# A twelve-layer decoder on one core: masks on diagonal blocks in one attention, squares halved on GpSimd, context keys begun sooner, and two side streams that both move at each place

## The chip, the cores and the metric

The kernel runs on one core of one Trainium2 chip. The metric is device microseconds of one execution; lower is better. Engines are named as in the profile: PE (TensorE matmul), PEld (its weight loads), DVE (VectorE), ACT (ScalarE), POOL (GpSimd), SP (SyncE, which issues most DMAs).

## The reference

The input x is 8 batches of 256 rows of 256 numbers; a context of 8 x 77 rows goes with it. Four layers follow, each of an attention, a cross-attention over the context and a feed-forward part, and each part ends in `x = layernorm(x + part(x))`. Only these parts matter here:

```
L1 attention: 16 heads of 16, causal; softmax(mask(q k^T / 4)) v, then a projection
L2 ffn:       a shared expert and routed experts
L3 attention: a state-space block: rmsnorm, in-projection, a causal convolution of 4 taps,
              chunks with decay exp(cumsum), then
              y = rmsnorm(y * silu(z)) ; out = y @ Wo + residual
L3 cross:     q = softmax over each head's 16 numbers; k likewise over the context's keys;
              out = q + (q @ k^T v) / (q . sum k), then a projection
L3 ffn:       up (256 to 1024), gelu, down (1024 to 256); the butterflies are folded into up and down
```

## The kernel before

A builder class writes one straight program; a scheduler underneath then orders the instructions of each engine nearly as they were written, moving one ahead only where its model finds the engine free. Every engine then works through its queue in order. All big matmuls are `mm` (line 169 in the profile), whatever layer they belong to. `ps()` hands out one of 8 PSUM banks of 512 f32 columns.

**Pieces.** Work that is to lie beside other work is written as Python generators: each `yield` ends a piece. `later` queues a generator on `todo`, and `tick` takes its next piece. `side` takes pieces from two more queues, `sides[0]` and `sides[1]`; it is called at places that are written into the main thread by hand. Before, one call took one piece, from the two queues in turn, or from the one that had work.

**L1's attention** (`l1_attn`). For a batch, `shift` computes scores by queries to get each row's maximum: for query half t (0: 128 keys, 1: 256 keys) and groups g of heads, four banks `ps[j]` hold the scores of head rows j. `weights` computes them again by keys (key half c) for the exponents, `weigh` applies them to v. The causal mask is added by a matmul of constants in bf16. Before, it came first and covered all columns of the bank: `later` is 128 columns of zeros followed by the causal matrix, `unit` is an identity followed by zeros, both 256 wide. `mats(gs, n)` is four banks. At t = 1 and at c = 0 there are two groups a batch with two heads of 256 columns, at t = 0 and c = 1 one group with four heads of 128. L0's attention in the same kernel (`by_queries`, `by_keys`, lines 636 and 662) writes the mask last and on the diagonal block alone.

**The end of L2 and L3's keys** (`rest` in `l3_attn`). L2's shared expert for blocks 2 and 3 is 34 pieces. Between them come L3's context keys, one generator `l3_keys` a batch (a matmul, a softmax that goes over DVE, ACT, DVE and POOL, then two small matmuls a half and their masking). `key` begins batch b and ends batch b - 1. `need` at given pieces asks for the routed experts' results (gathers on POOL's DMA queue). `fill(n)` takes n pieces of `rest` between the first steps of L3's attention; `for _ in more` drains what is left after `inputs(0, ...)`.

**L3's loop** goes over the 8 batches b. A turn is `tick`, `weights(b)` (decay matrices: `sel` matmuls on line 2193, relu, G, exp, the transposes of line 2226 for xd), `inputs(b + 1)` (Wx matmuls, convolution on DVE, Wz matmuls, silu), then `outputs(b)` goes on `todo`. There are 14 places for `side` in a turn. `outputs` gates y by z, squares it on ACT (line 2261), sums the 512 squares of each row by matmuls with a column of ones (`onec`), takes the rsqrt, projects and norms; its last piece writes XT and queues `cross(b)` on `sides[0]`. `cross` is q and its softmax (`head_softmax`, lines 2438 to 2444), the transposes of q (2306), the product with the keys, a transpose back (2329), the projection with `renorm`, and the transposes of the new x (2349); its end queues `dense(b)` on `sides[1]`: four up pieces with gelu, two down pieces, and the last norm and the store. The text calls these c.q, c.qT, c.kv, c.oT, c.wp, c.xT and d.up0 to d.up3, d.down0 and d.down1, with the batch's number. After the loop, `while self.todo or ...` takes a `tick` and side pieces until nothing is left.

Of the kernel before, what the change touches and what calls it, by code (L numbers as in the profile page):

```python
# [20 lines left out]
P = 128  # L21
# [40 lines left out]
class Build:  # L62
    def __init__(self, tc, a, ctx):
        self.tc, self.nc, self.a = tc, tc.nc, a
        self.n = 0
        self.flip = 0
        pool = lambda name, bufs=1, **kw: ctx.enter_context(tc.tile_pool(name=name, bufs=bufs, **kw))
        self.const = pool("const")
        self.xp = pool("xp", 2)
        self.wp = pool("wp", 5)  # L70
        self.sm = pool("sm", 4)
        self.tmp = pool("tmp", 3)
        self.psp = pool("ps", 8, space=PSUM)
        self.dr = pool("dr", 1, space=DRAM)
        self.keep_stack = ctx.enter_context(ExitStack())
        self.open_keep = lambda: self.keep_stack.enter_context(tc.tile_pool(name="keep", bufs=1))
        self.keep = None
        self.X = [None] * NT
        self.XT = [None] * NBLK
        self.late = lambda: pool("late", side="right")  # L80
        self.l3w = None
        self.n_slot_sets = 0
        self.todo = []
        self.sides = [[], []]
        self.turn = 0
        self.l1kT = None
        self.results = None
        self.routed = None
        self.slots = {}
        self.ms = {}  # L90
# [12 lines left out]

    def side(self, n=1):

        for _ in range(n):
            live = [q for q in (self.sides[self.turn], self.sides[1 - self.turn]) if q]
            if not live:
                return
            self.turn ^= 1  # L110
            if next(live[0][0], self) is self:
                live[0].pop(0)

    def wave(self):

# [1147 lines left out]
    def l1_constants(self):  # L1263
        nc, pool = self.nc, self.l1s_pool

        mxps, vps = [self.t(pool, [P, 4, 4, 32], f"mxp{t}") for t in range(2)], []
        for m in mxps:
            nc.gpsimd.memset(m, 0.0)
        for n in range(2):
            v = self.t(pool, [P, 2, H, 32], f"vp{n}")  # L1270
            nc.gpsimd.memset(v, 0.0)
            nc.gpsimd.memset(v[:, :, :, 16:17], 1.0)
            vps.append(v)
        later = self.t(pool, [P, 2 * P], "later", BF)
        nc.vector.memset(later[:, :P], 0.0)
        nc.vector.tensor_copy(later[:, P:], self.causb)
        unit = self.t(pool, [P, 2 * P], "unit", BF)
        nc.vector.tensor_copy(unit[:, :P], self.identb)
        nc.vector.memset(unit[:, P:], 0.0)
        self.l1c = mxps, vps, later, unit  # L1280

    def l1_attn(self):
        nc, a = self.nc, self.a
        with ExitStack() as ctx:
# [4 lines left out]
            Wp = self.load_w(a["L1_attn_Wp"], 2, 256)  # L1289
            self.slot_rows(2)  # L1290
            bk, bq = self.fm("l1_bk"), self.fm("l1_bq")
            mxps, vps, later, unit = self.l1c
            rows = [slice(32 * j, 32 * j + 32) for j in range(4)]
            many = lambda m, n: m.unsqueeze(1).to_broadcast([P, n, m.shape[1]])
            mats = lambda gs, n: [self.ps()[:, : len(gs) * n].rearrange("p (g s) -> p g s", s=n) for j in range(4)]
# [30 lines left out]
            def shift(b, q, k):  # L1326

                q2 = self.t(w2, [P, 4, S], "q2", bufs=1)
                for t in range(2):
                    n = P * (t + 1)  # L1330
                    mxp = mxps[t]
                    for gs in ((0, 1, 2, 3),) if t == 0 else ((0, 1), (2, 3)):
                        ps = mats(gs, n)
                        for j in range(4):
                            nc.tensor.matmul(ps[j], self.identb, many(later[:, 2 * P - n :], len(gs)), start=True, stop=False)
                        for i, g in enumerate(gs):
                            for j, r in enumerate(rows):
                                nc.tensor.matmul(
                                    ps[j][:, i, :], q[r, g, t * P : (t + 1) * P], k[r, g, :n], start=False, stop=(g == gs[-1])
                                )  # L1340
                        for j in range(4):
                            self.mark = nc.vector.tensor_reduce(
                                mxp[:, gs[0] : gs[-1] + 1, j, 16], ps[j], AX.X, ALU.max, negate=True
                            )
                        self.tick()
                for t in range(2):
                    pt = self.ps().rearrange("p (g s) -> p g s", g=4)
                    for g in range(4):
                        nc.tensor.transpose(pt[:, g, :], mxps[t][:, g].rearrange("p j d -> p (j d)"), self.ident)
                    c = slice(t * P, (t + 1) * P)  # L1350
                    nc.vector.tensor_tensor(q2[:, :, c], pt, q[:, :, c], ALU.add)
                return q2

            def weights(q2, k):

                e = {}
                for c, gs in ((0, (0, 1)), (0, (2, 3)), (1, (0, 1, 2, 3))):
                    n = S - c * P
                    ps = mats(gs, n)
                    for j in range(4):  # L1360
                        nc.tensor.matmul(ps[j], self.causb, many(unit[:, :n], len(gs)), start=True, stop=False)
                    for i, g in enumerate(gs):
                        for j, r in enumerate(rows):
                            nc.tensor.matmul(
                                ps[j][:, i, :], k[r, g, c * P : (c + 1) * P], q2[r, g, c * P :], start=False, stop=(g == gs[-1])
                            )
                    o = self.t(w2, [P, 4, len(gs), n], "e", bufs=3)
                    for j in range(4):
                        nc.scalar.activation(o[:, j], ps[j], AF.Exp, scale=0.25)
                    for i, g in enumerate(gs):  # L1370
                        e[c, g] = o[:, :, i, :]
                    self.tick()
                return e
# [618 lines left out]
    def l3_attn(self):  # L1992
        nc, a = self.nc, self.a
        with ExitStack() as ctx:
# [6 lines left out]
            def rest():  # L2001

                keys, n, b = {}, 0, 0

                def key():
                    nonlocal b
                    if b < NB:
                        keys[b] = self.l3_keys(w4, b, Wkv, bkv, mask)
                        next(keys[b])
                        yield  # L2010
                    if b:
                        for _ in keys.pop(b - 1):
                            pass
                        yield
                    b += 1


                due = {(2, 8): 0, (2, 12): 1, (2, 16): 2, (3, 4): 3, (3, 8): 4, (3, 14): 5, (3, 16): 6}
                for blk in (2, 3):
                    for k, _ in enumerate(self.l2_shared(w4, blk, self.l2r)):  # L2020
                        if (blk, k) in due:
                            self.gates.append(self.mark)
                            self.need(due[blk, k])
                        yield
                        n += 1
                        if n >= 13 and n % 4 == 1:
                            yield from key()
                while b <= NB:
                    yield from key()
# [210 lines left out]
            def outputs(b, cv, zs, E, xd):  # L2240
# [18 lines left out]
                sq = zs  # L2259
                for h in (slice(0, 2), slice(2, 4)):  # L2260
                    nc.scalar.activation(sq[:, h, :], y[:, h, :], AF.Square)
                yield
                p2 = self.ps()
                for t in range(2):
                    self.mm(p2[:, t : t + 1], [(sq[:, c, t * P : (t + 1) * P], onec) for c in range(4)])
                r2 = self.t(self.sm, [P, 2], "r2")
                nc.vector.tensor_copy(r2, p2[:, :2])
                self.rsqrt(r2, r2, 1.0 / 512, 1e-5)
# [19 lines left out]
            def cross(b):  # L2288
# [9 lines left out]
                for t in two:  # L2298
                    x = self.X[2 * b + t]
                    nc.gpsimd.tensor_tensor(x, x, bp, ALU.add)  # L2300
                yield
                yield
                ps = self.ps()
                for t in two:
                    for k in range(2):
# [2 lines left out]
                        )  # L2308
                qT = self.t(w5, [P, 4, P], "qT", bufs=1)
                nc.scalar.copy(qT, ps.rearrange("p (k n) -> p k n", k=4))  # L2310
                yield
                for t in two:
                    ps = self.ps()[:, : 2 * 136].rearrange("p (g n) -> p g n", g=2)
                    for g in range(2):
# [3 lines left out]
                    for g in range(2):  # L2318
# [3 lines left out]
                            z[:, g, :].unsqueeze(2).to_broadcast([P, 8, 16]),  # L2322
                            ALU.mult,
                        )
                yield
                ps = self.ps()
                for t in two:
                    for k in range(2):
# [1 line left out]
                            ps[:, (2 * t + k) * P : (2 * t + k + 1) * P], q[:, t, k * P : (k + 1) * P], self.ident  # L2330
                        )
                nc.vector.tensor_tensor(qT, ps.rearrange("p (k n) -> p k n", k=4), qT, ALU.add)
                yield
                ps = self.ps()
                for t in two:
                    self.mm(ps[:, t * D : (t + 1) * D], [(qT[:, 2 * t + k, :], Wqp[:, k, 256:]) for k in range(2)])
                for t in two:
                    x = self.X[2 * b + t]
                    nc.vector.tensor_tensor(x, ps[:, t * D : (t + 1) * D], x, ALU.add)
                    renorm(2 * b + t)  # L2340
                yield
                yield
                if b % 2 == 0:
                    xts[b // 2] = self.t(self.xp, [P, 2, 512], "xt", bufs=5)
                at = xts[b // 2][:, :, (b % 2) * S : (b % 2 + 1) * S]
# [8 lines left out]

            def dense(b, xT):
                up, bu, wd = self.l3w
                for t in range(2):
                    x = self.X[2 * b + t]
                    nc.gpsimd.tensor_tensor(x, x, bc, ALU.add)
# [66 lines left out]
                self.side()  # L2426
            while self.todo or self.sides[0] or self.sides[1]:
                self.tick()
                self.side(2)


    def head_softmax(self, q, n):
# [590 lines left out]
```

## Time and profile before

| what | us |
|---|---|
| median of 3 executions | 3451.7 (3451.05 to 3453.99) |
| the profiled execution's own time | 3455.78 |
| its span, first to last instruction | 3454.1 |
| PE busy in the span | 3062.8 (89%) |
| POOL busy in the span | 918.5 (27%) |

Times in the profile count from the span's start. L1's attention lies from about 1079 to 1320 us, the shared expert's last pieces and the context keys from about 2905 to 3022, L3's loop from 3022.7; its turns begin at 3022.7, 3047.0, 3079.2, 3133.5, 3183.9, 3238.3, 3286.9 and 3327.8 (the `sel` matmuls of line 2193), and the tail after the last turn runs from about 3347 to the end. An instruction's line can be that of a helper; then the operands tell which step it is (`ps<-onec,zs` is the sum of squares). A granted clock of 1.00 is PE at full rate.

### The profile page before, as it was taken

The numbers are of one execution on the slowest core, as the hardware profiler recorded it, in microseconds if no ns is written. First come the engines' busy times: TensorE is split into PE (matmuls) and PEld (weight loads), VectorE is DVE, ScalarE is ACT, GpSimd is POOL, SyncE is SP. The second block draws the span as 40 slices with busy tenths as digits, with TensorE's granted clock in tenths as the row PEclk, the third lists the DMA queues.
The fourth block names the chain that finished last, engine by engine and source line by source line (L and its number), as shares of the span: only waits on it lengthen the run. The fifth ranks groups of instructions, "written<-read, shape, count | busy, mean of one in ns | idle before, by whom it ended". The sixth has DMA issues, their size and how long they took to land. (4 is left out here: it accounts for less than half of the span.)

```text
span 3454.1 us, 49695 instructions
## 1 busy us (share of the span) xinstructions
PE 3062.8 (89%) x19263; PEld 2187.0 (63%) x19274; DVE 1825.2 (53%) x4839; ACT 1084.6 (31%) x2426; POOL 918.5 (27%) x1371
## 2 busy tenths in 40 slices
PE   4777679989998998998999999998787999889887
PEld 2444357768886666675555777565555786567776
DVE  7887556641105656785111221576675443676663
ACT  4666422222222233332111111344222112235342
POOL 2222323343313211232000000331343453423232
PEclk6777779989999999998999999999787999879999
DMA  9900110025532000001010333100001562000000
GB/s 334 336 1 2 37 43 14 18 85 193 183 135 89 13 31 15 14 20 59 14 37 0 129 129 118 46 21 8 6 21 68 177 221 98 27 7 4 4 7 13
DMA packets 132657, 239.96 MB, mean 69 GB/s; under 512 B 14584, under 2 KB 104448, under 8 KB 124736
## 3 DMA queue, kind: packets, MB, share of 16 engines
q1 hardware_dynamic: 108160, 136.71, 11.9%
q0 software_dynamic: 23104, 98.95, 8.4%
q8 instruction: 156, 2.56, 0.3%
q10 hardware_dynamic: 1152, 1.05, 0.1%
q14 instruction: 85, 0.70, 0.1%
HBM read 156.98 MB, written 79.69 MB: 69 GB/s over the span
## 5 line engine op out<-in xcount | busy, mean ns | idle before, releaser
L169 PE MATMUL ps<-xt,w 128*128 128x256 f32 (+1 forms) x1408 | 444.4, 465 | 8.4 <-issue 8.4
L169 PE MATMUL ps<-w,hT 128*128 128x256 f32 (+1 forms) x1792 | 397.4, 379 | 0.0
L169 PEld LDWEIGHTS ps<-w,hT 128*128 128x128 f32 (+1 forms) x1792 | 329.9, 186 | 56.5 <-issue 6.0
L169 PE MATMUL ps<-gT,w 128*128 128x256 f32 (+1 forms) x1472 | 357.1, 401 | 5.7 <-ACT gT L157 3.0
L169 PEld LDWEIGHTS ps<-xt,w 128*128 128x128 f32 x1408 | 263.2, 194 | 150.3 <-issue 129.5
L169 PEld LDWEIGHTS ps<-gT,w 128*128 128x128 f32 x1472 | 276.3, 191 | 76.7 <-ACT gT L157 3.9
L169 PE MATMUL ps<-w,oT 128*128 128x256 f32 x704 | 165.8, 391 | 1.1 <-ACT oT L157 0.2
L169 PEld LDWEIGHTS ps<-w,oT 128*128 128x128 f32 x704 | 135.1, 195 | 34.0 <-issue 11.1
L1160 ACT ACTIVATE hT<-ps,more 128x256 f32<-128x256 f32 x152 | 72.1, 474 | 199.2 <-PE ps L169 199.2
L1171 DVE COPY y<-ps 128x512 f32<-128x512 f32 x41 | 28.3, 690 | 174.6 <-PE ps L169 174.6
L1237 DVE TENSOR_TENSOR hT<-hT,ps 128x512 f32<-128x512 f32 x56 | 38.6, 689 | 149.8 <-PE ps L169 149.4
L699 ACT ACTIVATE e<-ps,nm 128x128 bf16<-128x128 f32 (+1 forms) x256 | 104.0, 462 | 39.6 <-DVE nm L694 23.9
L289 POOL TENSOR_TENSOR xb<-x,rows 128x256 f32<-128x256 f32 x80 | 61.4, 774 | 190.7 <-DVE res L294 187.8
L277 DVE TENSOR_SCALAR x<-res,mv,rs 128x256 f32<-128x256 f32 x112 | 53.2, 475 | 109.9 <-POOL rs L197 109.9
L1233 ACT ACTIVATE hT<-ps 128x512 f32<-128x512 f32 x56 | 33.4, 597 | 237.7 <-PE ps L169 237.7
L249 PE MATMUL ps<-ident,x 128*128 128x128 f32 x288 | 56.4, 308 | 58.1 <-DVE x L277 43.2
L1730 POOL TENSOR_TENSOR kpad<-kpad,rows 128x256 f32<-128x256 f32 (+1 forms) x10 | 7.3, 730 | 363.5 <-DVE hu L1679 276.2
L983 PE MATMUL ps<-PT,V 77*64 77x256 f32 x512 | 93.8, 425 | 6.9 <-ACT PT L157 4.4
L916 POOL TENSOR_TENSOR P<-P,z 128x1232 f32<-128x1232 f32 (+1 forms) x32 | 55.2, 1736 | 167.6 <-DVE z L915 167.6
L1594 ACT ACTIVATE f<-ps,neg 128x512 f32<-128x512 f32 x128 | 77.4, 689 | 57.2 <-PE ps L1591 57.2
L1595 DVE SCALAR_TENSOR_TENSOR f<-ps,f 128x512 f32<-128x512 f32 x128 | 79.1, 680 | 25.7 <-ACT f L1594 25.7
L968 PEld LDWEIGHTS ps<-ident,P 128*77 128x77 f32 x512 | 59.4, 153 | 50.8 <-issue 23.8
(674 smaller groups left out, 6435.1 us busy)
## 6 DMA issues: line engine op xcount, KB each, us to landing
l2x<-zero SPq DMA_DIRECT2D x28, 1024.0 KB, 11.3
l0x<-zero SPq DMA_DIRECT2D x16, 1024.0 KB, 11.4
w<-in_L_ffn_rg SPq DMA_DIRECT2D x8, 1024.0 KB, 7.0
w<-in_L_ffn_ru SPq DMA_DIRECT2D x8, 1024.0 KB, 5.1
w<-in_L_ffn_rd SPq DMA_DIRECT2D x8, 1024.0 KB, 5.6
l2e<-y SPq DMA_DIRECT2D x22, 256.0 KB, 2.3
l0e<-y SPq DMA_DIRECT2D x19, 256.0 KB, 2.9
w<-in_L_xattn_Wk SPq DMA_DIRECT2D x4, 1024.0 KB, 4.9
```

Of the source, the lines that this page charges most:

```text
L169: self.nc.tensor.matmul(out, lhsT, rhs, start=(i == 0), stop=(i == last))
L249: self.nc.tensor.transpose(ps[:, k * P : (k + 1) * P], x[:, k * P : (k + 1) * P], self.ident)
L277: nc.vector.tensor_scalar(t, r, mv[:, 0:1], rs, ALU.subtract, ALU.mult)
L289: self.nc.gpsimd.tensor_tensor(t, self.X[i], row, ALU.add)
L699: nc.scalar.activation(e[:, : (t + 1) * P], ps[j][:, i, :], AF.Exp, bias=nm[:, t, h : h + 1], accum_out=z[:, t, h : h + 1],)
L916: eng.tensor_tensor(pr, pr, z.unsqueeze(2).to_broadcast([P, n, SC]), ALU.mult)
L968: nc.tensor.transpose(psv[:, m, t * P : (t + 1) * P], Pt[t][:, 2 * n + m, :], self.ident)
L983: nc.tensor.matmul(po[64 * m : 64 * m + 64, :S], V[:, h * 64 : (h + 1) * 64], ahead[n % 2][:, m, :], start=True, stop=True,)
L1160: nc.scalar.activation(hT[:, f + m, :], ps[:, m * 256 : (m + 1) * 256], func, bias=more[:, f + m : f + m + 1])
L1237: nc.vector.tensor_tensor(hT[:, f, :], hT[:, f, :], ps, ALU.mult)
L1594: nc.scalar.activation(f[:, j], ps[j], AF.Exp, bias=neg1)
L1595: self.mark = nc.vector.scalar_tensor_tensor(f[:, j], ps[j], 1.0, f[:, j], ALU.max, ALU.min)
```

## The change

Four edits that do not touch one another:

- `side` advances both queues by one piece at each place, and is called once in the final loop instead of taking two pieces. `cross` gets more empty pieces between its steps (14 pieces in all, where there were 8), `dense` one at its start (9 where there were 8).
- In `outputs`, GpSimd adds the second half of the squares to the first, and the matmuls with `onec` take two blocks of 128 where they took four.
- In `rest`, a key step follows every third piece of the shared expert from the 13th on, where it followed every fourth.
- In L1's attention the mask matmul comes last and covers only the block on the diagonal; `later` and `unit` go.

```diff
     def side(self, n=1):
-        for _ in range(n):
-            live = [q for q in (self.sides[self.turn], self.sides[1 - self.turn]) if q]
-            if not live:
-                return
-            self.turn ^= 1
-            if next(live[0][0], self) is self:
-                live[0].pop(0)
+        for q in self.sides * n:
+            if q and next(q[0], self) is self:
+                q.pop(0)
...
         # l1_attn, shift
-                        for j in range(4):
-                            nc.tensor.matmul(ps[j], self.identb, many(later[:, 2 * P - n :], len(gs)), start=True, stop=False)
                         for i, g in enumerate(gs):
                             for j, r in enumerate(rows):
                                 nc.tensor.matmul(
-                                    ps[j][:, i, :], q[r, g, t * P : (t + 1) * P], k[r, g, :n], start=False, stop=(g == gs[-1])
+                                    ps[j][:, i, :], q[r, g, t * P : (t + 1) * P], k[r, g, :n], start=(i == 0), stop=False
                                 )
+                        for j in range(4):
+                            nc.tensor.matmul(
+                                ps[j][:, :, t * P : n], self.identb, many(self.causb, len(gs)), start=False, stop=True
+                            )
...
         # l1_attn, weights
-                    for j in range(4):
-                        nc.tensor.matmul(ps[j], self.causb, many(unit[:, :n], len(gs)), start=True, stop=False)
...
+                    for j in range(4):
+                        nc.tensor.matmul(
+                            ps[j][:, :, :P], self.causb, many(self.identb, len(gs)), start=False, stop=True
+                        )
...
         # l3_attn, rest
-                        if n >= 13 and n % 4 == 1:
+                        if n >= 13 and n % 3 == 1:
                             yield from key()
...
         # outputs
                     nc.scalar.activation(sq[:, h, :], y[:, h, :], AF.Square)
+                nc.gpsimd.tensor_tensor(sq[:, :2, :], sq[:, :2, :], sq[:, 2:, :], ALU.add)
                 yield
...
-                    self.mm(p2[:, t : t + 1], [(sq[:, c, t * P : (t + 1) * P], onec) for c in range(4)])
+                    self.mm(p2[:, t : t + 1], [(sq[:, c, t * P : (t + 1) * P], onec) for c in range(2)])
...
         # cross: after c.q, c.qT, c.kv, c.oT and c.wp
-                yield
-                yield
+                yield from (None,) * 4
...
-                yield
+                yield from (None,) * 2
...
-                yield
+                yield from (None,) * 2
...
-                yield
+                yield from (None,) * 2
...
-                yield
-                yield
+                yield from (None,) * 3
...
             def dense(b, xT):
                 up, bu, wd = self.l3w
+                yield
...
             while self.todo or self.sides[0] or self.sides[1]:
                 self.tick()
-                self.side(2)
+                self.side()
```

More of the change, by code (lines that the diff above doesn't have):

```diff
@@ L84, in __init__ @@
         self.sides = [[], []]
-        self.turn = 0
         self.l1kT = None
@@ L1273, in l1_constants @@
             vps.append(v)
[L1274 to L1280, printed above, removed]
+        self.l1c = mxps, vps
     def l1_attn(self):
@@ L1291, in l1_attn @@
             bk, bq = self.fm("l1_bk"), self.fm("l1_bq")
-            mxps, vps, later, unit = self.l1c
+            mxps, vps = self.l1c
             rows = [slice(32 * j, 32 * j + 32) for j in range(4)]
@@ L1364, in weights @@
                             nc.tensor.matmul(
-                                ps[j][:, i, :], k[r, g, c * P : (c + 1) * P], q2[r, g, c * P :], start=False, stop=(g == gs[-1])
+                                ps[j][:, i, :], k[r, g, c * P : (c + 1) * P], q2[r, g, c * P :], start=(i == 0), stop=False
                             )
+                    for j in range(4):
+                        nc.tensor.matmul(
+                            ps[j][:, :, :P], self.causb, many(self.identb, len(gs)), start=False, stop=True
+                        )
                     o = self.t(w2, [P, 4, len(gs), n], "e", bufs=3)
```

## The prediction

> **What bounds the kernel now.** I read the page's engine line first, then busy time in stretches, then PE's waits.
>
> ```profile
> PE 3062.8 (89%) x19263; PEld 2187.0 (63%) x19274; DVE 1825.2 (53%) x4839; ACT 1084.6 (31%) x2426; POOL 918.5 (27%) x1371
> ```
>
> PE is the busiest engine, but 89% is an average over stages, so each edit is priced in its own stretch: L1's attention, the end of L2, then the first seven turns of L3's loop and the tail. Columns: stretch, length, busy us of PE, PEld, DVE, ACT, POOL, granted clock, DMA share, GB/s.
>
> ```profile
> 1090.00:1300.00 210.00, 203.70 (x1979) 142.39 (x1981) 127.82 (x277) 64.12 (x136) 47.41 (x80) 1.00 0.08 24
> 2925.00:2998.00 73.00, 63.68 (x254) 43.82 (x253) 46.98 (x152) 24.41 (x36) 32.71 (x52) 0.93 0.11 31
> 2998.00:3022.70 24.70, 18.19 (x69) 12.18 (x68) 15.62 (x56) 3.24 (x6) 12.34 (x22) 0.71 0.08 22
> ```
>
> ```profile
> 3022.70:3047.00 24.30, 22.83 (x113) 19.10 (x112) 19.20 (x55) 9.39 (x18) 0.79 (x2) 0.71 0.08 23
> 3079.20:3133.50 54.30, 44.90 (x261) 39.03 (x259) 38.33 (x99) 23.24 (x36) 13.90 (x22) 0.87 0.00 1
> 3183.90:3238.30 54.40, 46.17 (x249) 38.18 (x248) 35.71 (x101) 19.58 (x34) 14.82 (x24) 0.91 0.02 6
> 3347.20:3454.00 106.80, 85.10 (x425) 72.08 (x424) 39.80 (x112) 22.50 (x42) 26.56 (x53) 0.94 0.03 10
> ```
>
> ```profile
> 3020.00:3040.00 20.00, 20.00 (x90) 17.29 (x91) 13.48 (x36) 8.56 (x17) 2.14 (x4) 0.62 0.09 27
> ```
>
> L1 is PE-bound (97% at full clock): PE work taken away there should come off the time. L3 is not: in turn 2 (3079.2 to 3133.5), turn 4 and the tail PE stands still for 8 to 22 us, and no other engine is full. What it waits for from 3020 us on (us in all, times, the longest):
>
> ```profile
> PE ps L2306 <- POOL q L2444: 25.4, 7, 8.1
> PE ps L2349 <- DVE x L2286: 6.2, 5, 2.5
> PE ps L169 <- DVE qT L2332: 5.4, 4, 2.9
> PE ps L169 <- DVE xt L155: 5.3, 3, 3.5
> ```
>
> All four are `cross` and `dense` pieces, queued on PE sooner than their input is made; the first is the turning of q after its softmax.
>
> **L1's masks.** 192 mask matmuls are 48 groups of four. The 32 groups of t=1 and c=0 shrink from 512 columns to 256; 16 keep 512. Both sizes stand in the trace, in L0's attention:
>
> ```profile
> 332.41 0.61 PE L662 MATMUL ps<-identb,causb 128*128 128x256 bf16 x4
> 332.95 1.06 PE L647 MATMUL ps<-qT,kd 32*128 32x512 bf16 x4
> ...
> 337.63 1.04 PE L662 MATMUL ps<-identb,causb 128*128 128x512 bf16 x4
> 338.60 0.53 PE L628 MATMUL ps<-kd,qT 32*128 32x128 bf16 x16
> ```
>
> Start to start, a group is 0.54 against 0.97 us: 0.43 x 32 = 13.8 us less. The mask now comes after the scores; ahead of them it could run while the scores' inputs were still being written, but PE then had the value projection to do, and L1335 itself idles 2.7 us in all: 2.7 is what lost cover can cost. Queued behind the later mask on PE are the next group's scores; who waits for it are the maxima on DVE and the exponents on ACT, which start on a bank once its own mask is done. What can eat the gain is DVE: twelve maxima a batch follow one another at about 0.61 us, 7.3 us, then two q2 adds of 0.68. If that chain sets the end of `shift`, its half (6.9 us) is lost. Bounds -6.9 to -13.8; PE idles only 0.9 us in 30, so I take -12. The two constants dropped are four small DVE instructions in L0's ffn, hidden by PE work; uncovered, under 1 us.
>
> **Squares.** 128 records of 128x1 become 64. Sixteen last from 3142.10 to 3143.81, 0.107 us each: 6.8 us less PE. Added are 8 GpSimd adds of 128x512 f32; the nearest row is L2257, same engine and shape, 1.27 us, 10.2 us in sum. An add queues ahead of the small rsqrt instructions that a norm waits for, and `p2`'s matmuls wait for it, with up3 and xd's transposes queued behind them on PE; between the squares and `p2` lie up1, G's matmuls and up2 (1.8 + 0.8 + 1.8 us of PE), which cover 1.27 us unless ACT is late with the squares. POOL is busy 12 to 16 us of a 50 us turn. Bounds -6.8 to +3.4 (all on the path, 10.2 - 6.8); I take -4, nearer the PE rows.
> Such an operation takes 0.689 us on DVE (L1237, one input from PSUM), 1.27 on POOL. The Trainium skill (GPSIMD Engine Reference, 4.1 Engine selection) speaks against this edit: plain adds belong on VectorE, GpSimd being about twice as slow. By that choice the upper bound would be 5.5 - 6.8 = -1.3 instead of +3.4.
>
> **Context keys.** `rest` has 50 steps either way, 37 taken before `inputs(0)`, 13 drained after it. Before, the last shared-expert step is number 45, and two beginnings and three closings of keys follow with nothing beside them; afterwards it is 47, and one beginning and two closings follow. That is the stretch 2998 to 3022.7: kv matmuls at 3009.48, 3014.43 and 3019.19, 4.9 us a body, PE idle 6.5 us. One body moves to the stretch 2925-2998, where PE has 9 us free; a body's PE work there is 1.9 + 2 x 0.6 = 3.1 us. The last gathers on POOL are issued two steps later, behind one more memset and multiply (0.7 us); block 1 needs them at 3020. So -2 to -5 directly; +2 if the shared steps, now later, hold up the `l2s` space that turn 0 writes. Turn 0 follows at clock 0.71; if the denser stretch kept the clock up, 24.3 x 0.29 = 7 us more. Bounds +2 to -12; I take -4.
> The row from 3020 to 3040 shows PE busy 20.00 of 20 us and still at 0.62. The Trainium skill (TensorE: Matmul & The Clock Gate, What's actually happening) has the full clock return after one busy window of about 3.4 us, which this row contradicts. By the page a cold start of turn 0 would cost about 1.7 us, and the lower bound would be -7.
>
> **Side pieces.** Before, 14 places a turn serve 16 pieces (8 of cross, 8 of dense) one at a time; after, each place serves both streams, cross being 14 pieces with its empty ones and dense 9. I wrote both orders out by hand. Work moves between turns: turn 2 loses dense 0's four up pieces (1.77 us each) and one down (3.5), 10.6 us; turns 3 to 5 hold a full dense each, +3.5 each; turn 7 takes 11.7 us from the tail (d4's up2, up3 and both downs, 10.6, and c5's kv, 1.1). That sums to zero, so only stalls count. Between c.q and c.qT stand now up0, up1, G, up2, p2, up3 and one xd: 7.1 + 0.8 + 0.9 + 0.6 = 9.4 us of PE. The softmax takes 7.4 (q done 3405.25, L2306 at 3412.67). So L2306's waits go, but not the first (8.1; no dense in turn 2): -17.3. Dense starts a whole score phase after its xt: -6.8 (5.3 DVE, 1.5 ACT). qT's waits in the loop: -4. L2349's stay. New: from `outputs`' projection to its transpose, cover falls from 6.4 us (c.wp 2.0, two Wx pieces 3.8, c.oT 0.6) to 4.4 (c.wp comes later), and the norm chain takes 4.4 (3156.2 to 3160.6): +1 in six turns, +6. In the tail, c6's and c7's renorm lose the down matmuls that cover them, 3.5 each: +7. The stores stay behind dense's last piece on an empty SP queue. Sum -15; -28 if nothing new appears, +29 at worst (rival 3).
>
> **Sum.** -12 - 4 - 4 - 15 = -35 against this execution's 3455.8 (span 3454.1): 3420.8. Its median over three is 4.1 lower, 3451.7, so 3417.
>
> **Rivals.**
> 1. *Stalls change place* (25%): L3's waits reappear at norm chains and PSUM evictions; L1, squares and keys remain: -20, 3432. For it: every chain passes DVE, POOL and DVE again; against: 25.4 us sit at one place.
> 2. *The clock rises too* (12%): turns 1 to 7 and the tail lose some 33 us to clocks of 0.87 to 0.99 (each stretch's length times one less its clock); with fewer pauses a third comes back, -11, and turn 0 runs warm, -7: 3399.
> 3. *Slower* (10%): the moved dense work lands in turns that are full, and leaves a turn and a tail that chains set. Turns 3 to 5 grow by 10.5 and turn 7 by 11.7 while turn 2 stays 54.3 and the tail 106.8, plus 7 for the bare renorms: +29 against -20, 3461. It decides if turn 2 and the tail together shrink by less than about 10 us. Against it: the tail holds 85 us of PE work of which 11.7 leaves.
> 4. *Keys do nothing* (within the others): the drain still ends in serial bodies; +4.
>
> **Numbers.** Forecast 53%, rivals as given. The range goes from rival 2 with L1 and squares at their low bounds (3399 - 1.8 - 2.8) to rival 1 with L1, squares and keys less good (L1 at -6.9 is +5, squares at +3.4 is +7, keys at -2 is +2): 3394 to 3446. Rival 3 lies outside. About 0.2%, 7 us, is what a measurement can tell from none. Faster 0.84, same 0.06, slower 0.10.
>
> **To check afterwards.** L1335 and L1361's successors with 64 records of 256 columns and a batch 1.5 us shorter; 64 records at `onec`; PE's wait at L2306 under 10 us in all; turn 2 near 45 us, turns 4 and 5 at 47 to 51; fewer kv waits before L3's first scores. It is wrong if PE's total wait in L3 does not fall, or if L1's period stays near 31 us because DVE took over.

## The result: no difference that can be measured

The changed kernel takes 3451.5 us (median of 12 executions, 3447.6 to 3456.4), the kernel before 3451.4 on the same chip (12 executions). The ratio is 0.9997, with a 95% interval of 0.9988 to 1.0006. Forecast were 3417 us and a range of 3394 to 3446. The profiled execution of after took 3453.26 us (span 3451.5), that of before 3455.78.

The page's engine line shows what was taken out and put in: PE has 64 records and 4 us less, POOL eight instructions and 14 us more.

```profile
PE 3058.7 (89%) x19199; PEld 2186.5 (63%) x19210; DVE 1828.4 (53%) x4835; ACT 1082.8 (31%) x2426; POOL 932.6 (27%) x1379
```

Busy time in stretches of after, columns as in the prediction: L1's attention, the end of L2, turn 2, turn 4, the tail.

```profile
1090.00:1290.00 200.00, 196.88 (x1984) 147.66 (x1985) 126.42 (x276) 64.76 (x137) 46.83 (x80) 0.99 0.08 25
2991.00:3022.10 31.10, 20.70 (x82) 14.94 (x80) 18.96 (x64) 8.39 (x11) 12.60 (x23) 0.77 0.06 18
3075.30:3117.30 42.00, 33.75 (x194) 27.88 (x192) 34.38 (x89) 14.65 (x24) 15.25 (x21) 0.83 0.00 1
3172.10:3218.80 46.70, 43.90 (x255) 37.47 (x252) 34.70 (x93) 20.05 (x34) 14.68 (x24) 0.96 0.02 6
3339.20:3451.40 112.20, 83.09 (x373) 67.88 (x371) 38.52 (x108) 19.57 (x37) 27.92 (x54) 0.88 0.03 10
```

Turn 2 went from 54.3 to 42.0 us and turn 4 from 54.4 to 46.7, as foreseen. But the stretch before L3's first scores, 24.7 us before, is 31.1, and the tail is 112.2 us where it was 106.8, with 52 matmul records fewer in it and a clock of 0.88 instead of 0.94.

What PE waits for from 3018 us to the end (us in all, times, the longest; lines of after are 5 to 8 lower than before's: L2299 is c.qT, L2341 c.xT, L244 the transposes after `outputs`' norm).

```profile
PE ps L2341 <- DVE x L2280: 12.7, 7, 3.0
PE ps L164 <- DVE qT L2325: 8.4, 4, 2.5
PE ps L2299 <- POOL q L2437: 7.7, 3, 6.2
PE ps L244 <- DVE x L272: 7.7, 5, 2.6
PE ps L310 <- POOL xb L2063: 6.6, 2, 3.6
PE ps L164 <- POOL zs L2255: 6.2, 2, 3.7
PE ps L2341 <- DVE mv L263: 5.2, 2, 2.6
```

The softmax wait fell from 25.4 to 7.7 us. Yet the whole list adds up to 61.3 us, where before's over the same stretch adds up to 59.7: other waits took its place.

Matching the two traces at the same instructions says where time went. After is 10.4 us ahead at L1's last score by keys, 7.4 after the entry into L1's cross-attention, 7.0 at the last silu of layer 2's routed experts (2891 us before), but only 0.6 at L3's first `sel`; 8.0 at the last exponent of the loop, and 2.6 at the end. So L1 gave 7 to 10 us, the stage of the keys cost 6.4, the loop gave 7, the tail took 5. These are two single executions; the runs below put intervals on them.

### The profile page after: what moved, and what is told of

Read it like the earlier page. It is cut to its first block, busy times and chain, and to the rows that moved or that the text cites. A ratio compares the mean times of both kernels' runs of the same rounds, so it can differ in the third digit from the quotient of the medians.

```text
span 3451.5 us, 49595 instructions
## 1 busy us (share of the span) xinstructions
PE 3058.7 (89%) x19199; PEld 2186.5 (63%) x19210; DVE 1828.4 (53%) x4835; ACT 1082.8 (31%) x2426; POOL 932.6 (27%) x1379
## 3 DMA queue, kind: packets, MB, share of 16 engines
q1 hardware_dynamic: 108160, 136.71, 11.9%
## 5 line engine op out<-in xcount | busy, mean ns | idle before, releaser
L244 PE MATMUL ps<-ident,x 128*128 128x128 f32 x288 | 57.3, 311 | 61.8 <-DVE x L272 46.9
```

Of the source, the lines that this page charges most:

```text
L244: self.nc.tensor.transpose(ps[:, k * P : (k + 1) * P], x[:, k * P : (k + 1) * P], self.ident)
```

## The experiments

Each edit was first made alone on the kernel before. Theory: each does what the prediction said, and something outside the sum ate the gain. Rival: some of the edits cost time themselves.

**L1's masks alone.** The edit of `l1_constants` and `l1_attn` as in the change, nothing else.

> L1's masks alone. Theory (the mask edit saves, other edits give it back): L1's batches shorten by 1.5 us, 7 to 10 us off the total, 3442 to 3445. Rival A (L1's saving is lost where L1's cross-attention begins, 2.4 us of it already are): under 4 us. Rival B (what the execution of after shows at the landmarks is clock chance): no difference in the median.

Ratio 0.9976 [0.9966, 0.9987], which on 3449.3 us is -8.3 us [-11.7, -4.5]. The mechanism is what was forecast. In L1's attention of after (PE's timeline: start, us, engine, line, operation) a group's mask of 256 columns goes start to start in 0.54 us, as L0's row promised.

```profile
1168.91 0.61 PE L1329 MATMUL ps<-causb,identb 128*128 128x256 bf16 x4
1169.45 1.15 PE L1325 MATMUL ps<-kT,qT 32*128 32x256 f32 x16
```

A batch's period (first score by keys to the next batch's) falls from 30.98 to 29.16 us in the steady batches. From the first score by keys to the last, L1 takes 207.3 to 207.5 us in the three profiled executions with this edit and 219.1 to 219.4 in the 13 others. Part of this comes back right behind it: from there to the second group of scores of L1's cross-attention it is 56.6 to 58.0 us against 54.9 to 55.9. In after the two longest waits there are those of before (2.78 and 5.18 us), but PE is busy longer, 47.1 against 43.7 us, at a granted clock of 0.88 against 0.94.

**Context keys alone.**

```diff
-                        if n >= 13 and n % 4 == 1:
+                        if n >= 13 and n % 3 == 1:
```

> Context keys after every third piece alone. Theory: the first scores of L3 wait for the last gathers of L2's routed results (their last norm on DVE and POOL ends at 3016.5 us before), which are issued behind two more key steps; from L2's end to L3's first scores 5 to 8 us longer, of which a warmer clock in turn 0 gives some back: 2 to 8 us slower. Rival A (as predicted, keys ended last): 2 to 5 us faster. Rival B: no difference.

1.0013 [1.0001, 1.0025]: +4.5 us [+0.3, +8.6], where -4 was forecast. The timeline of PE just before L3 shows one long wait that the kernel before does not have (its longest at these matmuls is 3.1 us). The idle time stands in brackets, with what ended it.

```profile
3010.87 2.01 PE L169 MATMUL ps<-kv 77*128 77x128 f32 x8 [7.63 <-DVE w L2474]
```

The small masking of a key on DVE (L2474) stood in DVE's queue behind two norms of gathered rows, which waited for POOL.

Two stretches show what the move brought: from the end of layer 2's last routed-expert silu on ACT to the end of the shared expert's last product, and from there to L3's first `sel`. First the kernel before, then this edit (columns as in the prediction):

```profile
2891.70:3004.60 112.90, 97.78 (x361) 64.35 (x360) 62.16 (x191) 35.49 (x55) 56.48 (x90) 0.91 0.21 65
3004.60:3022.70 18.10, 11.59 (x48) 8.04 (x47) 11.88 (x45) 3.24 (x6) 7.34 (x16) 0.68 0.03 8
2883.40:3001.20 117.80, 99.65 (x378) 66.01 (x378) 65.59 (x204) 40.07 (x60) 54.19 (x89) 0.93 0.19 60
3001.20:3015.50 14.30, 6.67 (x28) 4.97 (x26) 8.55 (x31) 1.09 (x3) 9.26 (x17) 0.68 0.10 28
```

The drain is 3.8 us shorter, as forecast for one body. The stretch that took the body in is 4.9 us longer, and PE's idle time in it grew by 3.0 us. In after these two are 123.1 and 14.4 us.

**Side pieces alone.** `side`, `cross`, `dense` and the final loop as in the change.

> Both side streams at each place, with the wider spacing, alone. Theory (the waits change place): PE's waits for q's softmax fall from 25 to under 10 us, those for renorm and qT rise from 12 to over 20; turns 2 to 6 gain 6 to 10 us and the tail gives 6 to 9 back; within 4 us of before. Rival (the forecast's): 10 us or more faster.

0.9994 [0.9982, 1.0006]: -2.1 us [-6.2, +2.1]. In the stretch from the last turn's first `sel` to the end, first before, then with this edit, both executions hold the same matmuls but for four transposes:

```profile
3327.80:3454.10 126.30, 99.94 (x518) 84.20 (x516) 53.96 (x140) 34.24 (x62) 35.25 (x64) 0.94 0.03 11
3317.20:3452.40 135.20, 106.53 (x514) 86.55 (x512) 52.95 (x137) 36.93 (x64) 32.49 (x58) 0.88 0.02 8
```

Of the 8.9 us more, 6.6 are busy time of PE and 2.3 idle time. Six other profiled executions with the tail of before take 124.2 to 130.2 us here, after takes 134.4. The loop ahead of it takes 293.0 us where it took 305.1; 4.2 us of that lie in turn 0, which holds no side piece, so the edit gained about 8 there. PE's waits that grew, first two of before that the prediction does not show, then with this edit (L2342 is c.xT there):

```profile
PE ps L249 <- DVE x L277: 4.1, 3, 2.0
PE ps L315 <- POOL xb L2070: 2.8, 2, 2.6
```

```profile
PE ps L2342 <- DVE x L2281: 12.0, 7, 3.0
PE ps L244 <- DVE x L272: 8.5, 6, 2.6
PE ps L164 <- DVE qT L2326: 8.4, 4, 2.5
PE ps L310 <- POOL xb L2065: 6.7, 2, 4.1
PE ps L2342 <- DVE mv L263: 5.3, 2, 2.6
```

**Squares alone.** The GpSimd add, and row sums over two blocks.

> The GpSimd add alone. Theory (POOL's add now ends last before the row sums: in after PE waits 6.2 us for it, most of it in the tail): between 2 us faster and 3 us slower. Rival (the forecast's): 4 us faster, all of the 6.8 us of PE work less what is lost.

1.0014 [1.0003, 1.0026]: +4.8 us [+1.0, +9.0]. PE's wait for the squares, first before, then with this edit:

```profile
PE ps L169 <- ACT zs L2261: 1.9, 2, 1.7
PE ps L169 <- POOL zs L2262: 6.4, 3, 3.6
```

PE waits for the add at three of the eight batches (0, 3 and 6) and not at the other five.

The four single edits sum to -8.3 + 4.5 - 2.1 + 4.8 = -1.1 us; the whole change, at 0.9997, is -1.0. Each term is uncertain by about 4 us, but nothing outside the edits is needed to explain the result: at best estimate two of the four cost what the masks brought.

**The tail with its old spacing.** The loop keeps the changed spacing, the final loop gets that of before.

```diff
+            self.tail = True                      # when the loop over b is over
             while self.todo or self.sides[0] or self.sides[1]:
                 self.tick()
-                self.side()
+                self.side(1 if all(self.sides) else 2)
...
-                yield from (None,) * 4            # in cross: 4, 2, 2, 2, 3; dense 1
+                yield from (None,) * (2 if self.tail else 4)   # tail: 2, 1, 1, 1, 2; dense 0
```

> The sides edit alone, but with the spacing of before from the end of the loop on. Theory (the loop gains 7 to 10 us, and the tail gives them back because dense's down matmuls no longer cover cross's renorm): 6 to 10 us faster than before, 3440 to 3443, with PE's waits at the transposes after renorm in the tail back under 2 us. Rival (the loop's gain is not real, or what a turn gains the next one loses whatever the tail does): within 3 us of the sides edit alone, whose ratio was 0.9994.

0.9977 [0.9969, 0.9986]: -7.9 us [-10.7, -4.8], against -2.1 with the changed tail. In PE's timeline of after the two last batches stand still before the product with `Wqp` and before c.xT, each time for a chain of DVE that has nothing queued over it:

```profile
3391.53 1.99 PE L164 MATMUL ps<-Wqp,qT 128*128 128x256 f32 x8 [1.72 <-DVE qT L2325]
3396.53 0.64 PE L2341 MATMUL ps<-ident,x 128*128 128x128 f32 x2 [3.01 <-DVE x L2280]
...
3418.22 1.99 PE L164 MATMUL ps<-Wqp,qT 128*128 128x256 f32 x8 [1.72 <-DVE qT L2325]
3423.22 0.44 PE L2341 MATMUL ps<-ident,x 128*128 128x128 f32 x2 [3.00 <-DVE x L2280]
```

With the old spacing in the tail the same steps (L2343 is c.xT there) come without these waits (c.qT waits once there, 3.46 us):

```profile
3402.71 1.89 PE L165 MATMUL ps<-Wqp,qT 128*128 128x256 f32 x8
3407.89 0.38 PE L2343 MATMUL ps<-ident,x 128*128 128x128 f32 x2
3408.46 0.44 PE L2343 MATMUL ps<-ident,x 128*128 128x128 f32 x2 [0.19 <-DVE x L2282]
```

The clock moved with them. From the last turn's first `sel` to the end it is 0.94 before, 0.88 with the sides edit alone and 0.91 with the old tail (126.3, 135.2 and 127.9 us).

**Both streams without the spacing.** Only `side` and the final loop as in the change; `cross` and `dense` keep their 8 pieces.

> The kernel before with only half of the edit of the side pieces: both streams take a piece at each place, and once in the final loop, but cross keeps its 8 pieces and dense its 8, without the new empty ones. Theory A (the gain of the loop comes from the distance of c.q to c.qT in the queue; two pieces of cross now lie one dense piece and the main work of one place apart): the waits at the turning of q stay above 15 us, and the tail, packed denser, loses as it did: 3452 to 3458. Theory B (advancing both streams is what matters, the empty pieces only spread the tail): 3440 to 3447.

1.0165 [1.0146, 1.0184]: +57 us, far beyond either theory. The wait at c.qT, 25.4 us before, nearly trebles. Between c.q and c.qT lies only one empty piece, and every place now takes a piece of `cross`: in turn 3 PE has 0.8 us of work between them (G's two products) and then waits 11.9 us.

```profile
PE ps L2301 <- POOL q L2439: 71.1, 8, 11.9
```

So advancing both streams needs the spacing. The spacing with one stream at a time was not tried.

**The add on VectorE.**

```diff
-                nc.gpsimd.tensor_tensor(sq[:, :2, :], sq[:, :2, :], sq[:, 2:, :], ALU.add)
+                nc.vector.tensor_tensor(sq[:, :2, :], sq[:, :2, :], sq[:, 2:, :], ALU.add)
```

> The halved row sums with the add on VectorE instead of GpSimd. Theory (the row sums stand in PE's queue where the squares have just ended, so any step put between makes PE wait; the engine sets how long): the wait at the sums shrinks by the difference of the two adds (about 1.27 against 0.6 us), the time is between before and the GpSimd version: 0 to 4 us slower. Rival A (only GpSimd's slowness costs): 3 to 5 us faster than before, the PE work saved. Rival B (the slowing seen is clock chance): no difference from before.

1.0018 [1.0006, 1.0030], no better than on GpSimd. Groups of instructions (count, shortest/median/longest in ns, first and last start):

```profile
L2262 DVE TENSOR_TENSOR zs<-zs x8: 679/686/1268, 3044.7 to 3362.5; 128x512 f32<-128x512 f32 x8
```

The Trainium skill (GPSIMD Engine Reference, 4.1 Engine selection) has the add about twice as fast on VectorE. The row agrees, 0.69 us against 1.27 on GpSimd, but the time does not follow. PE still waits three times for the squares, 5.3 us in all where it was 6.4 with the add on GpSimd. The 1.1 us between them are less than these intervals can tell apart.

**Half of the squares, and the add twice.** Two cuts of the same edit separate its two sides. The first takes the sums over two blocks with no add; the second makes the add twice.

```diff
-                    self.mm(p2[:, t : t + 1], [(sq[:, c, t * P : (t + 1) * P], onec) for c in range(4)])
+                    self.mm(p2[:, t : t + 1], [(sq[:, c, t * P : (t + 1) * P], onec) for c in range(2)])
```

> The kernel before, but the row sums take only the first two of the four blocks of squares, and nothing is added: half of the squares is left out of the norm. This is the squares edit without its GpSimd add. Theory A (the edit lost because PE's queue waits for the add): with the add gone the removed PE work comes back whole, 64 matmuls of 0.107 us, so about 3442.4. Theory B (the removed matmuls lay in time that PE had to spare or that kept its clock up, so that taking them away gives nothing whatever the add does): 3448 to 3452, no different from before.

```diff
                 nc.gpsimd.tensor_tensor(sq[:, :2, :], sq[:, :2, :], sq[:, 2:, :], ALU.add)
+                nc.gpsimd.tensor_tensor(sq[:, :2, :], sq[:, :2, :], sq[:, 2:, :], ALU.add)
```

> The squares edit with its GpSimd add made twice, one after the other (the second adds the second half once more, so the sums are not the right ones); nothing else changes. Theory A (PE's queue waits for the add): a second add of about 1.26 us on each of 8 batches is 10 us more than the single add's 3454.6, so about 3465. Theory B (the add lies beside other work, the loss comes from elsewhere): 3454 to 3457.

Without the add: 0.9992 [0.9982, 1.0003], -2.8 us, so 6.8 us of PE work taken away bring 2.8 at best estimate; the interval, -6.2 to +1.0 us, includes no gain at all and leaves out the whole 6.8. With two adds: 1.0041 [1.0026, 1.0057], +14. From none to one add the step is 0.0022, 7.6 us, from one to two 0.0027, 9.3 us, where eight adds last 10.2. By the intervals each step is uncertain by some 5 us or more; both together, 16.9 of 20.3 us, say that most of the adds' time reaches the end. PE's direct waits explain part of that. Its waits in L3, first with half the squares, then with two adds:

```profile
PE ps L2306 <- POOL q L2444: 27.6, 7, 7.3
```

```profile
PE ps L169 <- POOL zs L2263: 13.0, 4, 4.9
```

Where only PE work went, the wait for the softmax grew from 25.4 to 27.6 us: in L3 part of the saved matmuls ran while a chain elsewhere was the later one. From the first `sel` to the end PE's busy time fell there from 364.3 to 358.6 us, while its idle time rose from 67.1 to 71.0. The wait for the squares is 1.9 us before, 6.4 with one add and 13.0 with two, so PE's direct waits for the adds grew by 4.5 and then by 6.6 us. With two adds PE is also busy longer for the same matmuls than with one, 368.4 against 360.2 us, at a clock of 0.88 against 0.90. What makes up the rest was not settled.

**Where the keys may stand.** Four more orders of the same key steps, two of them to test the long wait.

```diff
-                        if n >= 13 and n % 4 == 1:
+                        if 13 <= n <= 28 and n % 3 == 1:               # none late
+                        if n >= 13 and n % 6 == 1:                     # later
+                        if n in (13, 16, 19, 22, 25, 28, 33):          # sooner, one between the last two gathers
+                        if n in (13, 17, 21, 25, 29):                  # as before, without 33
```

> Six key steps after pieces 13, 16, ..., 28 of the shared expert and none after, so that its last piece is step 45 as before: keys sooner, but no more of them ahead of the last pieces. Theory (the loss of the keys edit comes from the keys that stand ahead of the last shared pieces and the gathers behind them): within 2 us of before. Rival (keys sooner as such cost, by their softmax chains between the shared pieces): 3 to 5 us slower, as with the keys edit.

> The kernel before with the context keys begun later: a key step after every sixth piece of the shared expert from the 13th on, instead of every fourth. The change went to every third and cost about 4.5 us. Theory A (each key step moved forward among the shared expert's pieces costs time): moving them back gains about as much, 3445 to 3446. Theory B (the prediction's: keys left over run one after another with nothing beside them, some 2 us of idle PE each): two more bodies are left over, 3453 to 3455. Theory C (order hardly matters, and the loss of 4 to 5 us was a shift in when PE is held at half rate): 3447 to 3452.

> The kernel before with key steps after pieces 13, 16, 19, 22, 25, 28 and 33 of the shared expert: sooner than before, as in the change, but with one step between the two last calls for the routed experts' results (ahead of pieces 32 and 34), as before. In the edit every-third a step followed the last call and none lay between the two; the trace then has one wait of PE of 7.6 us at the keys' small matmuls, for a DVE instruction queued behind the norms of the gathered rows. Theory A (that meeting is the loss): the wait is gone (longest under 4 us) and the time is back at the kernel before or a little better, 3446 to 3451. Theory B (keys sooner cost time as such): 3453 to 3456, as the every-third edit.

> The kernel before without the key step after piece 33 (steps after 13, 17, 21, 25 and 29; the others are drained after the shared expert): nothing lies between the two last calls for the routed experts' results, and a key step follows the last. Theory A (that meeting is the loss): one wait of about 7 us appears at the keys' small matmuls, and the time is 3453 to 3457. Theory B (what counts is how many bodies are left to be drained, about 2 us each): one more body, 3451 to 3453, and no wait above 4 us.

In that order: 1.0011 [1.0000, 1.0022], 1.0020 [1.0010, 1.0031], 1.0012 [1.0001, 1.0022] and 1.0011 [1.0000, 1.0022] (the last two against 3479.4 us, which the kernel before took beside them). Sooner or later, all cost about 4 to 7 us, two of them with an interval that ends at no difference. A long wait at the keys' small matmuls for L2474 is there with steps at every third and every sixth piece (7.6 and 7.3 us) and with none late (6.5). Without piece 33 the longest is 4.7 us, and with one step between the gathers 2.7, at about the same cost. So that meeting is not the common cause, and my theory of it falls. What all have in common is PE standing still. From layer 2's last routed-expert silu on ACT to turn 0's first product with xd, PE is idle (length less the union of its records in the trace) for 22.8 to 25.3 us in all ten profiled executions with keys every fourth piece, and for 26.1 to 30.7 us in all six with another order. The two stretches shown above say how: a body costs time wherever it goes. In those ten executions they are 109.7 to 113.0 and 17.4 to 19.8 us. In the three with one body fewer to drain (every third piece, after, one between the gathers) they are 117.8 to 123.7 and 14.3 to 14.4; with two bodies more to drain (every sixth) 105.1 and 31.7, and with one more (without piece 33) 110.0 and 25.2. With none late, where as many are left as before, they are 115.1 and 20.3. Which queue decides in each was not settled.

**Masks and the better side pieces.** The masks, the changed spacing in the loop, the old one in the tail; keys and squares as before.

> L1's masks on the diagonal and the sides edit with the old spacing in the tail; keys and squares as before. Theory: the sum of the two, 8 us and 6 to 10 us, so 14 to 18 us faster than before, ratio 0.995 to 0.996. Rival (the sides edit brings nothing in any form): 8 to 10 us, ratio 0.997.

Median 3436.2 us; the ratio is 0.9958 [0.9944, 0.9972], which on 3449.2 us is 14.5 us less than the kernel before, and faster than both kernels: the sum of its two parts (-8.3 - 7.9 = -16.2) within the interval.

## Why the prediction was wrong, step by step

- **L1's masks: -12 forecast, -8.3 measured.** Right in mechanism, and -12 lies just outside the interval. L1 itself became 11.7 us shorter (219.1 to 207.4 from first to last score by keys), and a batch 1.8 us where 1.5 was forecast. One to three us came back at the entry into L1's cross-attention, where PE was slower and its longest waits the same; the sum had no term for that. DVE's maxima did not take over: PE is busy 196.88 of 200 us in the row above.
- **Squares: -4 forecast, +4.8 measured.** Two steps failed. "6.8 us less PE" was taken off the path, in a stage that the prediction itself had called not PE-bound: it was worth 2.8 at best estimate. And "which cover 1.27 us" held for five of the eight batches only: PE's wait for the squares grew from 1.9 to 6.4 us. The bound of +3.4 assumed that the PE time at least comes back; without that the upper bound is the add itself, +10.2. The upper bound of -1.3 for an add on VectorE failed in the same way: that kernel is slower than the one before, at 1.0018. The trace of before could have told where an add fits. There PE starts the sums 0.1, 9.7, 4.4, 0.8, 2.7, 3.0, 1.5 and 1.4 us after the squares of batches 0 to 7 end, so 1.27 us more do not fit at batches 0 and 3 and barely at 6 and 7. PE then waited at 0, 3 and 6.
- **Context keys: -4 forecast, +4.5 measured.** "One body moves" and its gain came true: the drain became 3.8 us shorter, within the 2 to 5. The step that failed is the price of the body where it went, "the stretch 2925-2998, where PE has 9 us free". That took it as free, because a body's 3.1 us of PE work fit into PE's idle time. Its steps also go through DVE, ACT and POOL, and the stretch that took it in became 4.9 us longer in the edit alone and 10.2 in after. The upper bound of +2 looked only at `l2s` space and so missed this. In the edit alone one wait behind the gathers' norms is visible; which queue decides in general stays open. The bound of -12 hoped for a warm turn 0. It took 19.8 us in after, but 20.1 to 24.3 in the ten profiled executions with the keys of before, so that can't be put down to the keys.
- **Side pieces: -15 forecast, -2.1 measured.** The gains came: L2306 from 25.4 to 6.4 us with this edit alone (-19.0, forecast -17.3), `dense`'s start from 6.8 to 0.8 (-6.0, forecast -6.8). What failed first is "qT's waits in the loop: -4": the waits at qT grew from 5.4 to 8.4 us, 7.0 us off the forecast. Then the waits at the transposes of `xb`, which the sum does not have, grew from 2.8 to 6.7, and "L2349's stay" was wrong by about 3: the waits at c.xT grew from 6.8 to 17.3, of which 7.6 are the tail's renorms, forecast as +7. The waits after `outputs`' norm grew from 4.1 to 8.5. That is near the forecast +6, but by luck: "+1 in six turns" gave 0.5 us in the loop, the rest came in the tail. Together +21.8 against -25.0: 3.2 us less where the sum said 15, and close to the -2.1 measured. The runs that differ only in the tail's spacing (0.9994 and 0.9977) lie 5.9 us apart at best estimate, near the +7 too. In the one pair of tails shown most of the loss is PE's slower work, 6.6 of 8.9 us, which was not priced.
- **The rivals.** Rival 1, stalls change place, is what happened in L3, and it was given 25%. But it kept L1, squares and keys as gains, and two of these were losses. Rival 2 went the other way: the span's clock is 0.908 against 0.913 in the two profiled executions. Rival 3 had the right place, a tail set by chains, and its condition was met: turn 2 and the tail together shrank by 6.9 us, less than 10. Its price for the loop was too high: turn 3 grew from 50.4 to 54.8 us, but turn 4 shrank from 54.4 to 46.7. "Keys do nothing" was the worst that was considered for the keys; they cost time.
- **The test that was written down.** "It is wrong if PE's total wait in L3 does not fall": it went from 59.7 to 61.3 us. The range's upper end took the side pieces at nothing, the squares at +3.4 and the keys at -2, inside their own bound of +2; with squares and keys both above their bounds at best estimate, the time lies 5 us above that end. That the four effects sum to no difference at all is chance.

## What to carry to other kernels

In a stage where PE stands still for chains, a saved matmul can be worth less than its duration, and an instruction put into a chain costs what it is longer than the time that was to spare there; read that time off the trace for every repetition, not for one. Work moved out of a serial drain is not free because the busiest engine has idle time where it goes: compare the length of both stretches. When a queue's spacing is changed, list for each consecutive pair of steps the work between them after the change, not only for the pair whose wait is to go, and treat the drain at the end as a schedule of its own. Try edits of such a bundle one by one: here their gains and losses summed to nothing, and the masks with the side pieces, whose tail kept its old spacing, gave 0.9958.

## What the runs showed of the hardware

PE's granted clock differs between executions of one code by enough to hide edits of this size. Turn 0 took 24.3 us at a clock of 0.71 in the profiled execution before, and 20.2 us at 0.92 in that of masks and better side pieces together, whose edits change nothing in that turn (no side piece exists yet); over the ten profiled executions with the keys of before it took 20.1 to 24.3. From the last turn's first `sel` to the end, seven executions of the same code took 124.2 us at 0.96 to 130.2 at 0.91. The two with the sides edit's tail lie outside that, 135.2 us at 0.88 and 134.4 at 0.89. In the first of the two PE needed 6.6 us more than in the kernel before for the same matmuls less four transposes. More idle time and a lower clock came together there; that the one brought the other is not shown.
